# Another order within a step: local attention and FFN of a gated block on one core

## The chip, the cores and the metric

One core of a Trainium2 chip runs the whole program. The metric is device time in microseconds (us). The engines are TensorE (PE, with PEld for its weight loads), VectorE (DVE), ScalarE (ACT), GpSimd (POOL) and SyncE (SP, which issues DMAs here). Each engine works its own queue in order, and they meet at semaphores.

## The reference

The input x (2 batches of 2048 tokens, 256 wide) is normalised and goes through two branches; the result is `x + s * silu(ffn)`. The branch s is global attention of 16 heads. The change concerns the second branch, two layers of local attention and a gated feed-forward network:

```python
def _layer(x, wqkv, qs, ksc, wo, lg, lb, w1, b1, w2, b2):
    h = shift_token(x)                       # half of the features one token later
    q, k, v = jnp.split(h @ wqkv, 3, axis=-1)     # 8 heads of 64
    q = l2norm(q) * qs
    k = l2norm(k) * ksc
    q, k = rotary_xpos(q, k)
    o = local_attention(q, k, v)             # window of 128 and the one before it
    x = x + o @ wo
    h = shift_token(x)
    h = (h - mu) / jnp.sqrt(var + 1e-05) * lg + lb
    a, g = jnp.split(h @ w1 + b1, 2, axis=-1)     # 682 each
    h = a * jax.nn.gelu(g, approximate=False)
    return x + h @ w2 + b2
```

All data are float32.

## The kernel before

`norms` and `global_attention` run first; they are not changed. `ffn_branch` (lines 422 to 899) is the last stage.

**Tiling.** A *slot* is 512 tokens of one batch in one layer: 2 layers x 4 chunks x 2 batches = 16 slots, numbered s, with the two batches in turn. A slot has four *steps* i = 0 to 3, each for one tile of 128 tokens. x lies transposed in `xA` (features on partitions), with one column ahead of it for the token shift.

**Pieces.** The order of all engines' queues is the order in which the Python code emits, under `manual_schedule`; waits between engines follow from the tiles. A *piece* is one function call. `piece(f)` calls it, then counts down a list `later`: `soon(n, f)` puts f there, and it is emitted behind the n-th piece after the one that asked for it (n = 0: right behind that one). `gates` holds functions that are emitted once in a step, ahead of the first `a_weights`.

**Attention of one tile.** `a_project(s, i, n)` (544) multiplies by wqkv: n = 0 is q, 1 is k, 2 is v. For v, ACT copies the result out. For q and k, ACT squares it (`sqq`, 567), DVE makes three products from the same PSUM bank (`rot`, `swp`, 573 to 575), POOL adds them (576), and two pieces later `norm` emits DVE's sum of squares and maximum (580, 584), POOL's power -1/2 (585) and POOL's scaling of `rot` (586). In the next step `a_turn` (590) transposes rot on PE; ACT copies q out, DVE copies k. `a_scores(hb)` (612) makes the scores of four heads (hb 0 or 1) in two banks; DVE adds the mask and takes the maximum (636); `weights` on ACT is four exponentials (645); `normalize`, a piece later, is DVE's reciprocal (651) and two products on POOL (`sm`, 654). `a_weights(hb)` (659) transposes sm on PE into two banks (`pw`, r = 0 and 1), copied to `pT` by ACT for r = 0 and DVE for r = 1. `a_sums(hb)` (678) multiplies by v (`po`); at hb 1 ACT copies to `oT`. `a_out` (700, `px`) multiplies by wo and DVE adds it to xA (`residual`, 520).

**FFN of one slot.** `f_mean` (713, `pm`) gives the mean by a matmul, DVE subtracts it (`hc`), ACT squares it (725). `f_var` (727, `pv`) is the mean of the squares; its `scale` is ACT's square root (735), DVE's reciprocal of 128x512 (736) and DVE's scaling of hc (740, 741). `f_gate(m, n)` (747, `pg`): twelve pieces, Gelu on ACT for n = 1, product on DVE for n = 0. `f_out(k, part)` (771): in layer 1 two halves of a sum (`py`) and a residual on DVE, in layer 2 `pz`, an addition, Silu, and the product and sum with the other branch.

**PSUM.** `bank` (452) gives out eight banks in turn. A bank that comes round again is written only when all that read its last contents are done.

**The loop** (833 to 899). In step (s, i) `cur` is the tile that is projected and `pre` the one of the step before, for which all attention is done. FFN work comes from slots s-1 (`a_out`, `f_mean`, `f_var`), s-2 (gates) and s-3 (`f_out`), as `xs` and `gs`:

| step | xs | gates |
|---|---|---|
| 0 | f_out half 0, parts 0 and 1 | 4 |
| 1 | a_out 0 and 1 | 2 |
| 2 | f_out half 1, parts 0 and 1 | 2 |
| 3 | f_mean, f_var | 4 |

The order in a step is: turn 0, turn 1 of pre; q of cur; scores 0; k of cur; first xs; scores 1; second xs; v of cur; `gates`; weights 0; a gate; weights 1; a gate; sums 0; other gates; sums 1. `load_1` and `load_2` bring the FFN weights of layer 2 on SP's queue behind steps (9, 3) and (10, 2); `load_qkv` ahead of (8, 0).

Of the kernel before, what the change touches and what calls it, by code (L numbers as in the profile page):

```python
# [18 lines left out]
P = 128  # L19
# [402 lines left out]
def ffn_branch(tc, t, xA, s_out, ident, eps_t, mean_w, vecs, b2_row, x_ch, out_ch):  # L422
# [8 lines left out]
    with ExitStack() as ctx:  # L431
# [13 lines left out]
        )  # L445
        mhalf = cp.tile([P, H2], F32, name="mhalf")
        nc.gpsimd.memset(mhalf, -0.5)
        ctx.enter_context(tc.manual_schedule())

        turn = [0]  # L450

        def bank(name, shape=(P, CH)):
            turn[0] += 1
            return psr.tile(list(shape), F32, tag=f"f{turn[0] % 8}", name=name)
# [4 lines left out]
        def soon(n, f):  # L459
            later.append([n, f])  # L460

        def piece(f):
            f()
            for x in later:
                x[0] -= 1
            due = [x for x in later if x[0] < 0]
            later[:] = [x for x in later if x[0] >= 0]
            for _, g in due:
                g()


        W = {}
# [71 lines left out]
        def a_project(s, i, n):  # L544

            l, b, cc = slots[s]
            nm = f"{s}_{i}_{n}"
            ti = cc * TPC + i
            ps = bank(f"pp_{nm}")
            for k in range(2):  # L550
                at = ti * P + (1 if k == 0 else 0)
                nc.tensor.matmul(  # L552
                    ps, xA[b][:, k, at : at + P], W["qkv"][:, k, n * INNER : (n + 1) * INNER],
                    start=(k == 0), stop=(k == 1),
                )
            if n == 2:
                v = pool.tile([P, INNER], F32, tag=f"v{b}", name=f"v_{nm}", bufs=3)
                nc.scalar.copy(v, ps)
                kvs[l, b, ti, "v"] = v
                if i == 0:  # L560
                    soon(0, lambda: release("a", b))
                return
            if n == 0:
                st[s, i] = {"ss": pool.tile([P, 2, H2], F32, tag="ss", name=f"ss_{nm}"), "rot": []}
            S = st[s, i]
            sq = pool.tile([P, INNER], F32, tag="sqq", name=f"sqq_{nm}")
            nc.scalar.activation(sq, ps, AF.Square)  # L567
            rot = pool.tile([P, H2, HD2], F32, tag=f"rot{n}", name=f"rot_{nm}")
            swp = pool.tile([P, H2, HD2], F32, tag="swp", name=f"swp_{nm}")
            src = ps.rearrange("p (h d) -> p h d", d=HD2)  # L570
            hf = HD2 // 2
            tcs, tsn = (W["rt", x, cc][:, i, n, None, :] for x in range(2))
            nc.vector.tensor_mul(rot, src, tcs.to_broadcast([P, H2, HD2]))  # L573
            nc.vector.tensor_mul(swp[..., :hf], src[..., hf:], tsn[..., :hf].to_broadcast([P, H2, hf]))
            nc.vector.tensor_mul(swp[..., hf:], src[..., :hf], tsn[..., hf:].to_broadcast([P, H2, hf]))  # L575
            nc.gpsimd.tensor_add(rot, rot, swp)  # L576
            S["rot"].append(rot)

            def norm():
                nc.vector.tensor_reduce(  # L580
                    S["ss"][:, n, :], sq.rearrange("p (h d) -> p h d", d=HD2), AX.X, ALU.add
                )
                rn = pool.tile([P, H2], F32, tag="rn", name=f"rn_{nm}")
                nc.vector.tensor_scalar_max(rn, S["ss"][:, n, :], 1e-24)  # L584
                nc.gpsimd.tensor_tensor(rn, rn, mhalf, ALU.pow)  # L585
                nc.gpsimd.tensor_mul(rot, rot, rn[:, :, None].to_broadcast([P, H2, HD2]))

            soon(1, norm)
# [23 lines left out]
        def a_scores(s, i, hb):  # L612
# [25 lines left out]
                        mx[:, hb, r, x : x + 1],  # L638
                    )

            def weights():
                for r in range(2):
                    sm = S["sm"][hb, r]
                    for x in range(2):
                        nc.scalar.activation(  # L645
                            sm[:, x, lo:], sm[:, x, lo:], AF.Exp, scale=-1.0,
                            bias=mx[:, hb, r, x : x + 1], accum_out=ls[:, hb, r, x : x + 1],
                        )

            def normalize():  # L650
                nc.vector.reciprocal(ls[:, hb], ls[:, hb])  # L651
# [1 line left out]
                    sm = S["sm"][hb, r][:, :, lo:]  # L653
                    nc.gpsimd.tensor_mul(sm, sm, ls[:, hb, r, :, None].to_broadcast([P, 2, 2 * P - lo]))  # L654

            soon(0, weights)
            soon(1, normalize)

        def a_weights(s, i, hb):
# [4 lines left out]
            for r in range(2):  # L664
# [4 lines left out]
                            ps[:, x, pa, :], S["sm"][hb, r][:, x, pa * P : (pa + 1) * P], ident  # L669
                        )  # L670
                pT = pool.tile([P, 2, 2, P], F32, tag="pT", name=f"pT_{s}_{i}_{hb}_{r}", bufs=4)
                if r == 0:
                    nc.scalar.copy(pT[:, :, p0:, :], ps[:, :, p0:, :])
                else:
                    nc.vector.tensor_copy(pT[:, :, p0:, :], ps[:, :, p0:, :])  # L675
# [37 lines left out]
        def f_mean(s):  # L713
# [8 lines left out]
            release("f", b)  # L722
            sq = pool.tile([P, 2, CH], F32, tag="sq", name=f"sq_{s}", bufs=1)
            fs[s] = {"hc": hc, "sq": sq, "u": []}
            soon(0, lambda: nc.scalar.activation(sq, hc, AF.Square))

        def f_var(s):
            l, b, cc = slots[s]
# [2 lines left out]
            for k in range(2):  # L731
                nc.tensor.matmul(pw, mean_w, sq[:, k, :], start=(k == 0), stop=(k == 1))
            rs = pool.tile([P, CH], F32, tag="rs", name=f"rs_{s}", bufs=1)
            def scale():
                nc.scalar.activation(rs, pw, AF.Sqrt, bias=eps_t)
                nc.vector.reciprocal(rs, rs)
                V = vecs[:, l, :]
                for k in range(2):
                    c0 = 2 * NM + k
                    nc.vector.tensor_mul(hc[:, k, :], hc[:, k, :], rs)  # L740
                    nc.vector.tensor_scalar(
                        hc[:, k, :], hc[:, k, :], V[:, c0 : c0 + 1], V[:, c0 + 2 : c0 + 3], ALU.mult, ALU.add
                    )

            gates.append(scale)

        def f_gate(s, m, n):

# [3 lines left out]
            mw = min(P, HID - m * P)  # L752
            at = n * HID + m * P
            hc = fs[s]["hc"]
            ps = bank(f"pg_{nm}")
            for k in range(2):
                nc.tensor.matmul(  # L757
# [71 lines left out]
        load_2(0)  # L829
        n_slots = len(slots)  # L830
        per_layer = B * NCH
        last = None
        for s in range(n_slots + 3):
            a = s if s < n_slots else None

            fo, fg, fy = (x if 0 <= x < n_slots else None for x in (s - 1, s - 2, s - 3))
            for i in range(TPC):
                if i == 0 and s % B == 0 and B <= s <= per_layer:
                    if s == B:
                        load_scales(1)  # L840
                    load_tables(1, s // B - 1)
                if i == 0 and s == per_layer:
                    load_qkv(1)
                xs = []
                if i in (0, 2) and fy is not None:
                    xs = [(lambda p=p, k=i // 2: f_out(fy, k, p)) for p in range(2)]
                if i == 1 and fo is not None:
                    xs = [(lambda k=k: a_out(fo, k)) for k in range(2)]
                if i == 3 and fo is not None:
                    xs = [lambda: f_mean(fo), lambda: f_var(fo)]  # L850
                gs = []
                if fg is not None:
                    for m in ((0, 1), (2,), (3,), (4, 5))[i]:
                        gs += [(lambda m=m, n=n: f_gate(fg, m, n)) for n in (1, 0)]
                cur = (a, i) if a is not None else None
                pre = last
                last = cur

                def run(q, n=1):
                    for _ in range(n):  # L860
                        if q:
                            piece(q.pop(0))

                if pre:
                    piece(lambda: a_turn(*pre, 0))
                    piece(lambda: a_turn(*pre, 1))
                if cur:
                    piece(lambda: a_project(*cur, 0))
                if pre:
                    piece(lambda: a_scores(*pre, 0))  # L870
                if cur:
                    piece(lambda: a_project(*cur, 1))
                run(xs)
                if pre:
                    piece(lambda: a_scores(*pre, 1))
                run(xs)
                if cur:
                    piece(lambda: a_project(*cur, 2))
                for g in gates:
                    g()  # L880
                gates.clear()
                if pre:
                    piece(lambda: a_weights(*pre, 0))
                run(gs)
                if pre:
                    piece(lambda: a_weights(*pre, 1))
                run(gs)
                if pre:
                    piece(lambda: a_sums(*pre, 0))
                run(gs, 4)  # L890
                if pre:
                    piece(lambda: a_sums(*pre, 1))

                if s == per_layer and i == 1:
                    load_o(1)
                if s == per_layer + 1 and i == 3:
                    load_1(1)
                if s == per_layer + 2 and i == 2:
                    load_2(1)


# [87 lines left out]
```

## Time and profile before

| | us |
|---|---|
| median of 3 runs | 3884.55 (3881.63 to 3889.24) |
| the profiled execution's own time | 3884.26 |
| its span | 3882.5 |
| last stage: first matmul of the FFN branch to the end | 2092.34 to 3882.5 |

The page gives the busy time of each engine over the span. A window line gives, for a stretch of time, its length, busy time of PE, PEld, DVE, ACT and POOL with the instructions in brackets, the clock granted to PE (1.00 is full), the DMA share and GB/s. A wait line reads: engine and line that waited, what it waited for, us in total, times, longest. A timeline line reads: start, us, engine, line, operation, output <- input, shapes, how many in the group, and in square brackets the idle time ahead of it with what ended it. Matmul ends are modelled, so the time from the start of a group to the start of the next is the better measure of its length.

### The profile page before, as it was taken

The page shows a single profiled execution, that of the slowest core. Times are in us where ns is not written, and L with a number is a line of the kernel's source. Part 1 is how long each engine was busy: PE and PEld are TensorE (multiplying, and loading weights), DVE is VectorE, ACT ScalarE, POOL GpSimd, SP SyncE. Part 2 cuts the span into 40 slices and gives each one's busy share as a digit, 9 for nine tenths or more (in the row PEclk, how much of TensorE's full clock was granted, in tenths as well). Part 3 has the DMA queues.
Part 4 walks back from the last instruction along what each step waited for, and adds up shares of the span by engine and source line. Part 5 has one row for each costly group of instructions (what it writes and reads, how often), then busy time and mean ns, then how long its engine had stood idle before and what let it go on. Part 6 is the DMA issues. An engine that isn't in the chain of part 4 may idle for free.

```text
span 3882.5 us, 56277 instructions
## 1 busy us (share of the span) xinstructions
PE 3564.7 (92%) x21856; PEld 1688.3 (43%) x21856; DVE 2334.0 (60%) x4894; ACT 2063.8 (53%) x4170; POOL 1156.3 (30%) x978
## 2 busy tenths in 40 slices
PE   2999999999999999999996778888989999999998
PEld 1534334334343343434432444444444445555554
DVE  8767777777777777777751444545444444444442
ACT  1166666666666666666663344444444444444452
POOL 4011111111111111111113544445444435454441
PEclk9699999999999999999997899999999999999999
DMA  2000000000000000000002000000000000000001
GB/s 72 4 1 1 1 1 1 1 1 1 12 6 7 1 1 1 1 1 1 1 12 79 1 6 1 6 1 6 1 22 6 1 28 9 17 17 17 17 9 44
DMA packets 26172, 40.44 MB, mean 10 GB/s; under 512 B 3806, under 2 KB 19122, under 8 KB 25906
## 3 DMA queue, kind: packets, MB, share of 16 engines
q1 hardware_dynamic: 24466, 34.08, 2.6%
q8 instruction: 172, 2.82, 0.3%
q10 hardware_dynamic: 1440, 2.77, 0.2%
q14 instruction: 94, 0.77, 0.1%
HBM read 28.46 MB, written 8.39 MB: 9 GB/s over the span
## 4 chain that ended last, share of the span: by engine, by line
PE 76%; DVE 11%; ACT 5%; POOL 5%; issue 2%; DMA 1%; ACTq 0%; POOLq 0%; SPq 0%; DVEq 0%
PE pm L280 16%; PE po L335 12%; PE ps L316 11%; PE pg L757 7%; PE pp L552 6%; PE po L689 4%; DVE mx L283 3%; PE px L704 3%; PE pz L800 2%; POOL sm L654 2%; PE pw L668 2%; PE px L374 2%; PE pt L598 2%; ACT sm L645 2%; PE pp_wk L232 2%
## 5 line engine op out<-in xcount | busy, mean ns | idle before, releaser
L283 DVE TENSOR_REDUCE mx<-pm 128x1 f32<-128x512 f32 x2048 | 1285.6, 683 | 450.9 <-PE ps L316 429.9
L322 ACT ACTIVATE e<-ps 128x512 f32<-128x512 f32 x2048 | 1059.4, 607 | 466.2 <-PE ps L316 345.0
L280 PE MATMUL pm<-kT,qT 32*128 32x512 f32 x4096 | 1148.8, 639 | 0.8 <-DVE mx L283 0.8
L316 PE MATMUL ps<-qa,kT 32*128 32x512 f32 x4096 | 1116.5, 627 | 5.7 <-ACT e L322 4.8
L345 POOL TENSOR_TENSOR o<-o,part 128x512 f32<-128x512 f32 x224 | 283.5, 1266 | 1580.6 <-ACT part L344 1580.6
L280 PEld LDWEIGHTS pm<-kT,qT 32*128 32x128 f32 x4096 | 432.4, 188 | 435.4 <-DVE mx L283 338.5
L335 PE MATMUL po<-e,v 128*32 128x512 f32 x4096 | 492.5, 598 | 0.0
L316 PEld LDWEIGHTS ps<-qa,kT 32*128 32x128 f32 x4096 | 390.9, 183 | 154.6 <-ACT e L322 62.5
L576 POOL TENSOR_TENSOR rot<-rot,swp 128x512 f32<-128x512 f32 x128 | 162.4, 1269 | 797.5 <-DVE swp L575 757.7
L552 PE MATMUL pp<-wqkv,xA 128*128 128x512 f32 x768 | 379.9, 618 | 14.4 <-DMA wqkv<-in_wqkv_dram 14.4
L757 PE MATMUL pg<-hc,w 128*128 128x512 f32 (+1 forms) x768 | 379.8, 629 | 0.0
L645 ACT ACTIVATE sm<-sm,wmx 128x256 f32<-128x256 f32 (+1 forms) x512 | 250.4, 490 | 171.9 <-DVE wmx L636 171.2
L654 POOL TENSOR_TENSOR sm<-sm,wls 128x512 f32<-128x512 f32 (+1 forms) x256 | 254.2, 1014 | 26.6 <-DVE wls L651 23.7
L335 PEld LDWEIGHTS po<-e,v 128*32 128x32 f32 x4096 | 106.9, 109 | 348.1 <-DVE mx L283 187.4
L573 DVE TENSOR_TENSOR rot<-pp,rt 128x512 f32<-128x512 f32 x128 | 88.5, 691 | 248.7 <-ACT sqq L567 230.4
L585 POOL TENSOR_TENSOR rn<-rn,mhalf 128x8 f32<-128x8 f32 x128 | 210.8, 1647 | 55.4 <-DVE rn L584 55.4
L344 ACT COPY part<-po 128x512 f32<-128x512 f32 x224 | 131.0, 585 | 167.0 <-PE po L335 167.0
L689 PE MATMUL po<-pT,v 128*64 128x128 f32 x1984 | 159.3, 301 | 55.8 <-DVE pT L675 55.8
L552 PEld LDWEIGHTS pp<-wqkv,xA 128*128 128x128 f32 x768 | 138.7, 197 | 154.3 <-issue 141.2
L668 PE MATMUL pw<-ident,sm 128*128 128x128 f32 x992 | 150.0, 288 | 60.6 <-POOL sm L654 59.7
L675 DVE COPY pT<-pw 128x512 f32<-128x512 f32 (+1 forms) x128 | 84.8, 672 | 195.5 <-PE pw L668 195.4
L757 PEld LDWEIGHTS pg<-hc,w 128*128 128x128 f32 (+1 forms) x768 | 132.9, 187 | 142.0 <-issue 141.3
(136 smaller groups left out, 3795.8 us busy)
## 6 DMA issues: line engine op xcount, KB each, us to landing
xt<-in_x_dram SPq DMA_DIRECT2D x8, 512.0 KB, 3.7
s_out<-s_all SPq DMA_DIRECT2D x8, 512.0 KB, 2.6
rt<-in_rot_dram SPq DMA_DIRECT2D x16, 256.0 KB, 4.6
s<-s_out SPq DMA_DIRECT2D x16, 256.0 KB, 3.4
x<-in_x_dram SPq DMA_DIRECT2D x16, 256.0 KB, 3.5
out_dram<-y SPq DMA_DIRECT2D x16, 256.0 KB, 2.2
wqkv<-in_wqkv_dram SPq DMA_DIRECT2D x4, 768.0 KB, 8.3
w<-in_w_dram SPq DMA_DIRECT2D x4, 682.0 KB, 5.5
```

What stands on the lines that cost most here:

```text
L280: nc.tensor.matmul(ps, qT[rows, q0 : q0 + P], kT[rows, c * CH : (c + 1) * CH], start=True, stop=True)
L283: nc.vector.tensor_reduce(mxs[n][:, i * GH + j, c : c + 1], ps, AX.X, ALU.max)
L316: nc.tensor.matmul(ps, kT[rows, kt * P : (kt + 1) * P], qas[n][rows, :], start=True, stop=True)
L322: nc.scalar.activation(e, ps, AF.Exp)
L335: nc.tensor.matmul(pos[n][j * HP : (j + 1) * HP, :], v[:, kt, j * HP : (j + 1) * HP], es.pop((n, kt, j)), start=(kt % 2 == 0), stop=(kt % ...
L345: nc.gpsimd.tensor_add(os[n], os[n], part)
L552: nc.tensor.matmul(ps, xA[b][:, k, at : at + P], W["qkv"][:, k, n * INNER : (n + 1) * INNER], start=(k == 0), stop=(k == 1),)
L645: nc.scalar.activation(sm[:, x, lo:], sm[:, x, lo:], AF.Exp, scale=-1.0, bias=mx[:, hb, r, x : x + 1], accum_out=ls[:, hb, r, x : x + 1],)
L654: nc.gpsimd.tensor_mul(sm, sm, ls[:, hb, r, :, None].to_broadcast([P, 2, 2 * P - lo]))
L668: nc.tensor.transpose(ps[:, x, pa, :], S["sm"][hb, r][:, x, pa * P : (pa + 1) * P], ident)
L689: nc.tensor.matmul(S["po"][r * HD2 : (r + 1) * HD2, c, :], kvs[l, b, kt, "v"][:, h * HD2 : (h + 1) * HD2], S["pT", hb, r][:, x, pa, :], st ...
L757: nc.tensor.matmul(ps[:mw], W["1"][:, k, at : at + mw], hc[:, k, :], start=(k == 0), stop=(k == 1))
```

## The change

The diff does the following.

- A step has another order: sums 1 of the tile two steps back (`pre2`); v of cur; turn 0 and 1 of pre; the first of xs; scores 0 of pre; q of cur; scores 1; k of cur; the rest of xs; `gates`; weights 0; gates; weights 1; gates; sums 0; gates.
- FFN work is dealt out anew. xs is f_var(s-2) in step 0, two a_out(s-1) in step 1, f_out(s-3) half 0 in step 2, f_out half 1 and f_mean(s-1) in step 3. The gates of s-2 are queued from step 1 on, 2, 3, 2 and, in step 0 of the next slot, 5.
- `f_var`'s function becomes `root` (square root on ACT at once), `invert` (the reciprocal in four quarters, 1, 3, 5 and 7 pieces on) and `scale(k)` (10 and 11 pieces on). If hc isn't scaled at a gate, `all_due` emits all that is pending.
- The exponentials are emitted within `a_scores`, which is where `soon(0, ...)` had put them.
- The addition of the rotation (576) goes from POOL to DVE; the maximum with 1e-24 (584) is taken against a constant tile `tiny` instead of an immediate.
- `pT` is copied by DVE for hb 0 and by ACT for hb 1.
- The pending column of xA (`release("a")`) is written two pieces after k is projected. `load_1(1)` and `load_2(1)` move to behind (10, 0) and (10, 3).
- The steps behind the last tile have a plan of their own.

```diff
-            nc.gpsimd.tensor_add(rot, rot, swp)
+            nc.vector.tensor_add(rot, rot, swp)
...
-                nc.vector.tensor_scalar_max(rn, S["ss"][:, n, :], 1e-24)
+                nc.vector.tensor_max(rn, S["ss"][:, n, :], tiny)
...
-                if r == 0:
+                if hb == 1:
                     nc.scalar.copy(pT[:, :, p0:, :], ps[:, :, p0:, :])
...
-            soon(0, lambda: nc.scalar.activation(sq, hc, AF.Square))
+            soon(1, lambda: nc.scalar.activation(sq, hc, AF.Square))
...
-            def scale():
+            def root():
                 nc.scalar.activation(rs, pw, AF.Sqrt, bias=eps_t)
-                nc.vector.reciprocal(rs, rs)
+                for q in range(TPC):
+                    soon(2 * q + 1, lambda q=q: invert(q))
+                soon(2 * TPC + 2, lambda: scale(0))
+                soon(2 * TPC + 3, lambda: scale(1))
+
+            def invert(q):
+                nc.vector.reciprocal(rs[:, q * P : (q + 1) * P], rs[:, q * P : (q + 1) * P])
...
+            if not fs[s].get("ready"):
+                all_due()
...
+                if i == 0 and have(s - 2):
+                    xs = [lambda: f_var(s - 2)]
+                if i == 1 and have(s - 1):
+                    xs = [(lambda k=k: a_out(s - 1, k)) for k in range(2)]
+                if i == 1 and have(s - 2):
+                    gq += gate_pieces(s - 2)
+                if i >= 2 and have(s - 3):
+                    xs = out_pieces(s - 3, i - 2)
+                if i == 3 and have(s - 1):
+                    xs = xs + [lambda: f_mean(s - 1)]
+                ng = (5, 2, 3, 2)[i]
...
+            if pre2:
+                piece(lambda: a_sums(*pre2, 1))
+            if cur:
+                piece(lambda: a_project(*cur, 2))
+            if pre:
+                piece(lambda: a_turn(*pre, 0))
+                piece(lambda: a_turn(*pre, 1))
+            run(xs)
+            if pre:
+                piece(lambda: a_scores(*pre, 0))
+            if cur:
+                piece(lambda: a_project(*cur, 0))
+            if pre:
+                piece(lambda: a_scores(*pre, 1))
+            if cur:
+                piece(lambda: a_project(*cur, 1))
+                if i == 0:
+                    soon(2, lambda: release("a", slots[s][1]))
+            run(xs, 9)
+            for g in gates:
+                g()
+            gates.clear()
+            if pre:
+                piece(lambda: a_weights(*pre, 0))
+            run(gq, (ng + 1) // 3)
+            if pre:
+                piece(lambda: a_weights(*pre, 1))
+            run(gq, (ng + 1) // 3)
+            if pre:
+                piece(lambda: a_sums(*pre, 0))
+            run(gq, ng - 2 * ((ng + 1) // 3))
```

More of the change, by code (lines that the diff above doesn't have):

```diff
@@ L447, in ffn_branch @@
         nc.gpsimd.memset(mhalf, -0.5)
+        tiny = cp.tile([P, H2], F32, name="tiny")
+        nc.gpsimd.memset(tiny, 1e-24)
         ctx.enter_context(tc.manual_schedule())
@@ L469, in piece, with all_due @@
                 g()
+        def all_due():
+            while later:
+                later.pop(0)[1]()
         W = {}
@@ L559, in a_project @@
                 kvs[l, b, ti, "v"] = v
-                if i == 0:
-                    soon(0, lambda: release("a", b))
                 return
@@ L639, in a_scores @@
                     )
[L641 to L648, printed above, removed]
+            for r in range(2):
+                sm = S["sm"][hb, r]
+                for x in range(2):
+                    nc.scalar.activation(
+                        sm[:, x, lo:], sm[:, x, lo:], AF.Exp, scale=-1.0,
+                        bias=mx[:, hb, r, x : x + 1], accum_out=ls[:, hb, r, x : x + 1],
+                    )
             def normalize():
@@ L654, in normalize @@
                     nc.gpsimd.tensor_mul(sm, sm, ls[:, hb, r, :, None].to_broadcast([P, 2, 2 * P - lo]))
-            soon(0, weights)
             soon(1, normalize)
@@ L733, in f_var, with scale @@
             rs = pool.tile([P, CH], F32, tag="rs", name=f"rs_{s}", bufs=1)
-            def scale():
+            def root():
                 nc.scalar.activation(rs, pw, AF.Sqrt, bias=eps_t)
-                nc.vector.reciprocal(rs, rs)
-                V = vecs[:, l, :]
[L738 to L745, printed above, removed]
+                for q in range(TPC):
[4 more added lines that the diff above has]
+                nc.vector.reciprocal(rs[:, q * P : (q + 1) * P], rs[:, q * P : (q + 1) * P])
+            def scale(k):
+                c0 = 2 * NM + k
+                V = vecs[:, l, :]
+                nc.vector.tensor_mul(hc[:, k, :], hc[:, k, :], rs)
+                nc.vector.tensor_scalar(
+                    hc[:, k, :], hc[:, k, :], V[:, c0 : c0 + 1], V[:, c0 + 2 : c0 + 3], ALU.mult, ALU.add
+                )
+                fs[s]["ready"] = k == 1
+            gates.append(root)
         def f_gate(s, m, n):
@@ L831, in ffn_branch @@
         per_layer = B * NCH
[L832 to L899, printed above, removed]
@@ new lines, in out_pieces, with gate_pieces, have, run @@
+        def out_pieces(s, k):
+            return [(lambda p=p: f_out(s, k, p)) for p in range(2)]
+        def gate_pieces(s):
+            return [(lambda m=m, n=n: f_gate(s, m, n)) for m in range(NM) for n in (1, 0)]
+        gq = []
+        tiles = [(s, i) for s in range(n_slots) for i in range(TPC)]
+        for n in range(len(tiles) + 4):
+            s, i = divmod(n, TPC)
+            cur, pre, pre2 = (tiles[x] if 0 <= x < len(tiles) else None for x in (n, n - 1, n - 2))
+            def have(x):
+                return 0 <= x < n_slots
+            xs = []
+            if s == n_slots:
+                if i == 1:
+                    xs = [lambda: a_out(s - 1, 0), lambda: a_out(s - 1, 1)] + out_pieces(s - 3, 0)
+                    xs += [lambda: f_mean(s - 1)]
+                    gq += gate_pieces(s - 2)
+                elif i == 2:
+                    xs = out_pieces(s - 3, 1) + [lambda: f_var(s - 1)]
+                elif i == 3:
+                    xs = []
+                else:
+                    xs = [lambda: f_var(s - 2)]
+                ng = (5, 2, 5, 5)[i]
+            else:
+                if i == 0 and have(s - 2):
+                    xs = [lambda: f_var(s - 2)]
+                if i == 1 and have(s - 1):
+                    xs = [(lambda k=k: a_out(s - 1, k)) for k in range(2)]
+                if i == 1 and have(s - 2):
+                    gq += gate_pieces(s - 2)
+                if i >= 2 and have(s - 3):
[3 more added lines that the diff above has]
+                ng = (5, 2, 3, 2)[i]
+            if i == 0 and s % B == 0 and B <= s <= per_layer:
+                if s == B:
+                    load_scales(1)
+                load_tables(1, s // B - 1)
+            if i == 0 and s == per_layer:
+                load_qkv(1)
+            def run(q, n=1):
+                for _ in range(n):
+                    if q:
+                        piece(q.pop(0))
+            if pre2:
[29 more added lines that the diff above has]
+            run(gq, ng - 2 * ((ng + 1) // 3))
+            if s == per_layer and i == 1:
+                load_o(1)
+            if s == per_layer + 2 and i == 0:
+                load_1(1)
+            if s == per_layer + 2 and i == 3:
+                load_2(1)
@@ L903, in _padded_heads @@
+        s = n_slots + 1
+        run(gq, 99)
+        for k in range(2):
+            run(out_pieces(s - 3, k), 2)
+        gq += gate_pieces(s - 2)
+        run(gq, 3)
+        for g in gates:
+            g()
+        gates.clear()
+        run(gq, 99)
+        for k in range(2):
+            run(out_pieces(s - 2, k), 2)
+        all_due()
+        for g in gates:
+            g()
+        gates.clear()
 def _padded_heads(w):
```

## The prediction

> **What bounds the kernel now.** First the page's busy line and the windows over the span, to find the stage; then who TensorE waited for, from 2085 us on; then TensorE's timeline over one chunk; last the clock in the two stretches behind the long gaps.
>
> ```profile
> PE 3564.7 (92%) x21856; PEld 1688.3 (43%) x21856; DVE 2334.0 (60%) x4894; ACT 2063.8 (53%) x4170; POOL 1156.3 (30%) x978
> ```
>
> ```profile
> 2800.00:3000.00 200.00, 183.32 (x909) 95.26 (x908) 95.37 (x279) 91.33 (x211) 94.58 (x81) 0.95 0.04 14
> ```
>
> The change touches only the last stage (2092 to 3882 us). In it TensorE (PE) is busy 183 of 200 us, VectorE (DVE) 95, ScalarE (ACT) 91, GpSimd (POOL) 95: PE sets the pace, the others are half idle and matter only where PE waits for them.
>
> ```profile
> PE pv L732 <- ACT sq L725: 65.9, 16, 4.3
> PE pw L668 <- POOL sm L654: 59.7, 50, 4.2
> PE po L689 <- DVE pT L675: 55.8, 15, 5.5
> ```
>
> Three waits hold nearly all PE idle time: pv and po once a slot, pw mostly in the first slots, where no FFN work covers the softmax.
>
> ```profile
> 2770.29 1.09 PE L598 MATMUL pt<-ident,rot 128*128 128x128 f32 x8
> 2771.22 1.88 PE L552 MATMUL pp<-wqkv,xA 128*128 128x512 f32 x4
> 2773.03 1.16 PE L623 MATMUL ps<-xT,xT 64*128 64x128 f32 x16
> ...
> 2775.95 1.88 PE L718 MATMUL pm<-xA,mean_w 128*128 128x512 f32 x4
> 2777.76 1.16 PE L623 MATMUL ps<-xT,xT 64*128 64x128 f32 x16
> 2783.24 3.51 PE L732 MATMUL pv<-sq,mean_w 128*128 128x512 f32 x4 [4.32 <-ACT sq L725]
> ...
> 2797.59 1.76 PE L689 MATMUL po<-pT,v 128*64 128x128 f32 x13 [3.59 <-DVE pT L675]
> ```
>
> ```profile
> 2783.00:2786.60 3.60, 3.37 (x5) 1.53 (x6) 1.82 (x10) 2.26 (x9) 3.52 (x4) 0.54 0.00 0
> 2797.00:2806.00 9.00, 8.40 (x42) 4.12 (x43) 2.54 (x4) 1.00 (x2) 0.00 (x0) 0.64 0.01 2
> ```
>
> Both gaps lie in step 3, and behind each the granted clock is 0.54 and 0.64: pv takes 3.34 us to the next group where pm takes 1.81.
>
> A slot lasts 107.1 us (px at 2304.98 and, 13 slots on, 3697.40). Groups in the timeline, start to start at full clock: pp 1.82, ps 1.09, pw 0.88, half a po 0.95, pt 0.93, pg 1.8, px 3.6, py 2.66 and 2.97, pm and pv 1.8. Times the counts of a slot (12, 8, 8, 8, 4, 12, 2, 2 and 2, 1 and 1): 92.7 us. The other 14.4 are idle (8.3% of 107, 8.8 us) and slow clock.
>
> **What the Trainium skill says.** "SBUF — State Buffer", section on the two separate sides: VectorE with two SBUF inputs and GpSimd share a port pair under an exclusive lock; the loser blocks for the whole instruction. The trace agrees for the maximum on line 584: 0.17 us alone, but 0.90 here, until the first POOL product ends:
>
> ```profile
> 2144.68 2.05 POOL L654 TENSOR_TENSOR sm<-sm,wls 128x512 f32<-128x512 f32 x2
> 2144.86 0.90 DVE L584 TENSOR_SCALAR rn<-ss 128x8 f32<-128x8 f32 x1
> ```
>
> "PSUM — Partial Sum Buffer", its summary of rules: guard PSUM by bank, not by address. The trace agrees: with DVE free, the first mask starts at 3771.09, 0.14 us after the last ps of its pair of banks ended (3769.47 + 1.48).
>
> ```profile
> 3769.47 1.48 PE L623 MATMUL ps<-xT,xT 64*128 64x128 f32 x16 [0.24 <-ACT xT L601]
> ...
> 3771.09 0.42 DVE L636 CUSTOM_DVE_ANT_0 sm<-ps,mask 128x256 f32<-128x256 f32 x1 [1.13 <-PE ps L623]
> ```
>
> "TensorE: Matmul & The Clock Gate", on oscillation: PE idle beyond about 3.4 us brings back the half clock. The trace shows it behind 4.32 and 3.59; behind some gaps of 3.44 in the first slots pw x8 takes 2.11 instead of 1.04, behind others not.
>
> **The change, part by part.** Removed: pv's wait (f_var comes a step after f_mean), and po's wait (the 3.35 us reciprocal is cut in four quarters between pieces, the scaling put later). That is 4.3 + 3.6 us and, by the groups behind them, 1.6 + 2.6 of slow clock: 12.1 a slot. The 1.1 us pw waits of steps 0 and 2 would be next.
>
> Edits that cost nothing by themselves: POOL's addition (1.27 us, 128 times) leaves an engine half idle; DVE gains two additions a step, 0.69 each by the SBUF product on line 740, on 13 of 27 us, so DVE is no throughput bound. The maximum against `tiny` stays near 0.17 us plus the lock. Copies of pT change engine by half instead of by pair: same count. Weight loads for layer 2 move, but their last use moves with them and 15 us or more of pieces lie before the first use, against 5.5 to 8.3 us to land; next on SP's queue are the s and x loads of the output, two steps or more later. Table products on POOL stand at the same step start, before sm.
>
> What costs is the order. ACT's queue in a step is now exp0, square q, exp1, square k; DVE's is mask0, rotate q and add, reciprocal 0, mask1, rotate k and add, reciprocal 1, then the second FFN or px piece's residual. Each hands to the other, so it is one chain. From the end of scores 0 on PE (t = 0), with gaps from the timeline:
>
> - mask0 0.14; exp table at 0.65 (1.3); four exps 1.97: square q at 3.92.
> - rotation 0.60 later, 4.52 (the trace shows DVE waiting for the square every time); three products 1.27; addition 0.63: reciprocal 0 at 6.43.
> - POOL starts 0.32 after it: the first half of sm0 at 7.8, the second at 8.8.
> - mask1 6.5, exp1 0.46 later, four exps: square k 8.95; rotation 9.55; addition 10.82. POOL then ends its power (1.65) and starts the q product (1.04): the lock costs 0 or 1.05; neither end is excluded, I take 0.5. It ends 11.95.
> - reciprocal 1 11.95; POOL: sm1 halves 13.3 and 14.35. A residual (0.74) comes after it: 12.8.
>
> And eight PSUM banks go round in order of allocation. Counted off the new loop: py is followed by two score banks, q, two, k, and two pw banks; the second pw bank of hb 0 is py's own (in step 3, with pm between, the first). In step 0 it is pv's, which is free when ACT's Sqrt, now queued behind square k, ends: 9.5 + 1.3 (table) + 0.69 (line 735) = 11.5. So these transposes wait for the residual or the root, not only for sm. Before, py's bank came back at hb 1, long free.
>
> PE's cover from t = 0 and its waits, by step:
>
> - step 0: q 1.8, scores 1.1, k 1.8 = 4.7. sm0 at 7.85: 3.15. Then 8.3 to 11.5: 3.2.
> - step 1: with px 3.6, 8.3. sm0 is there (0.1). With pw and one gate 11.0; sm1 at 13.35 and 14.4: 2.9.
> - step 2: with py 2.95, 7.65, 0.2 for sm0; at 8.3 the bank, 12.8: 4.5.
> - step 3: with py and pm 9.45; bank 12.8: 3.35. The next half of po waits 0.6 for ACT's pT, behind Square (1.06) and Gelu.
>
> Sum 18.0; a slot is 92.7 + 18.0 = 110.7. Three gaps or pairs are near or over the 3.4 us behind which the clock fell; 1.6 us each (pv's loss), I take two: 3.2. Slot 113.9, 6.8 more than now; 13 slots: +88.
>
> Ends: in slots 0 to 2 the new chain lacks the exp table load (t = 13.1 for sm1) and a step comes to 22 us, as now (22.05, 22.9, 21.8); f_mean's and the reciprocal's waits of slots 1 and 2 go, five gates move out, step 1 of slot 1 loses its px cover: −5. The tail from the last tile on: five gates more (9), 5 us for the first softmax, less wait elsewhere: 126 against 114, +12. Sum +95 on the profiled execution's span of 3882.5 us (its own time 3884.26, 0.3 below the median): 3979; I say 3980.
>
> **Rivals.** *Cover as now, step 3 gains* (the faster case): if sm1 were ready 11 us after scores 0, as early as PE gets there, the 12.1 and some 1.5 of pw waits go: 13 × 13.6 − 7 = −170, 3715. For it: half of DVE and ACT is idle. Against: their order, above; it decides if the chain is 3.4 us shorter, which needs squares and rotations not to be waited for. *Chain without slow clock, DVE wins the lock*: slot 109.2, +34, 3918. For it: gaps are split by short groups. *Banks free early* (the count or the order of residuals misread): waits for sm alone, 13.2, slot 105.9: −9, 3875. Against: residuals stand behind both rotations in DVE's queue. *VectorE as bound*: excluded above.
>
> **How the numbers follow.** Forecast 0.52, its own range 3920 to 4040; no slow clock 0.20; banks free 0.13; step 3 gains in full or part (3700 to 3860) 0.15. A change of 0.2% (8 us) is about what can be told from none. Slower: 0.52 + 0.20 + 0.02 = 0.74; same 0.05; faster 0.21. The range 3850 to 4050 leaves out most of the faster case (0.13) and 0.07 above, where both lock and clock fall out badly.
>
> **What would show it.** Right: pv and po nearly gone from PE's waits; pw the largest by far, some 250 to 290 us, released in step 0 by the Sqrt or POOL, in steps 2 and 3 by the residual (lines of xA), in step 1 by POOL; PE's clock below 0.95; DVE additions of 0.69 with some near 1.7. Wrong: pw waits below 1 us in steady slots, or a slot below 107 us.

## The result and the profile after

The changed kernel takes 4032.93 us (median of 4 runs, 4029.47 to 4034.97), the kernel before 3885.88 beside it: ratio 1.0378, 95% interval 1.0361 to 1.0394. It is 147 us slower; 95 were forecast. The profiled execution's span is 4033.2 us, 150.7 more than before.

The page's line of busy times of the kernel after:

```profile
PE 3623.5 (90%) x21856; PEld 1721.1 (43%) x21856; DVE 2464.4 (61%) x5070; ACT 2053.4 (51%) x4166; POOL 1001.6 (25%) x851
```

TensorE executes the same 21856 matmuls and is busy 58.8 us longer. The last stage in one window line each, first the kernel before, then after:

```profile
2091.00:3883.00 1792.00, 1588.11 (x8096) 877.40 (x8096) 833.17 (x2292) 797.09 (x1765) 812.22 (x688) 0.94 0.04 14
```

```profile
2091.00:4033.00 1942.00, 1648.07 (x8096) 910.86 (x8096) 964.08 (x2468) 786.74 (x1761) 657.46 (x560) 0.90 0.04 13
```

The stage is 150 us longer: PE idle grew from 203.9 to 293.9 (+90), and its 8096 matmuls took 60 us longer at a mean clock of 0.90 instead of 0.94. Those two numbers are the whole loss. VectorE is 131 us longer busy and GpSimd 155 us less, but both stand idle for about half of the stage or more; they count only where TensorE waits for them.

Who PE waited for, in the kernel after, on the weights transpose:

```profile
PE pw L670 <- POOL sm L657: 126.5, 69, 4.5
PE pw L670 <- DVE xA L536: 65.0, 16, 4.6
PE pw L670 <- DVE y L822: 35.9, 10, 4.2
PE pw L670 <- ACT rs L737: 24.1, 8, 3.1
PE pw L670 <- POOL rot L590: 17.0, 6, 3.1
```

The waits of pv (65.9) and po (55.8) are gone. What is left in the steady slots is pw: 268.5 us over the stage, against 59.7 before. The names xA (layer 1's residual), y (layer 2's addition) and rs (the square root) are no inputs of a weights transpose. They are the last readers of the bank that it is about to write. "POOL rot" in step 0 is such a case with a wrong name: the product on POOL ended at 2861.71, but so, within 0.2 us, did the square root (2861.56), and it is the root that reads the bank.

```profile
2860.67 1.04 POOL L590 TENSOR_TENSOR rot<-rot,rn 128x512 f32<-128x512 f32 x1
...
2860.87 0.69 ACT L737 ACTIVATE rs<-pv,eps_t 128x512 f32<-128x512 f32 x1
```

PE's timeline of the kernel after, over steps 2, 3, 0 and 1 in turn:

```profile
2790.14 1.16 PE L627 MATMUL ps<-xT,xT 64*128 64x128 f32 x16
2791.24 1.98 PE L558 MATMUL pp<-wqkv,xA 128*128 128x512 f32 x4
2793.15 1.16 PE L627 MATMUL ps<-xT,xT 64*128 64x128 f32 x16
2794.24 1.99 PE L558 MATMUL pp<-wqkv,xA 128*128 128x512 f32 x4
2796.07 2.93 PE L793 MATMUL py<-u,w 128*128 128x512 f32 x6
2799.16 0.66 PE L670 MATMUL pw<-ident,sm 128*128 128x128 f32 x4 [0.16 <-POOL sm L657]
2804.38 1.09 PE L670 MATMUL pw<-ident,sm 128*128 128x128 f32 x4 [4.56 <-DVE xA L536]
2805.26 3.62 PE L769 MATMUL pg<-hc,w 128*128 128x512 f32 x4
...
2835.50 1.06 PE L670 MATMUL pw<-ident,sm 128*128 128x128 f32 x8 [3.60 <-DVE xA L536]
2836.40 3.14 PE L769 MATMUL pg<-hc,w 128*128 128x512 f32 x4
...
2857.91 1.12 PE L670 MATMUL pw<-ident,sm 128*128 128x128 f32 x4 [2.93 <-POOL sm L657]
2861.70 1.09 PE L670 MATMUL pw<-ident,sm 128*128 128x128 f32 x4 [2.67 <-POOL rot L590]
2862.58 6.09 PE L769 MATMUL pg<-hc,w 128*128 128x512 f32 x8
...
2897.44 0.65 PE L670 MATMUL pw<-ident,sm 128*128 128x128 f32 x4 [2.32 <-POOL sm L657]
2898.44 1.12 PE L670 MATMUL pw<-ident,sm 128*128 128x128 f32 x4 [0.34 <-POOL sm L657]
2899.35 3.07 PE L769 MATMUL pg<-hc,w 128*128 128x512 f32 x4
```

Every step now ends its projections with a gap ahead of pw: together 16.6 us in the slot shown (16.2 on average over twelve). Behind each, four pg that take 1.8 us at full clock take 2.9 to 3.4, and eight, 3.4 at full clock, take 5.9. A slot (pm to pm, from 2471.80 to 3893.43 over twelve) is 118.5 us; before it was 107.0. Twelve slots give 137 of the 150.7 us, the ends 13.

The chain behind the 4.56 us gap of step 2, from the timeline of the kernel after, all engines:

```profile
2791.34 0.42 DVE L640 CUSTOM_DVE_ANT_0 sm<-ps,mask 128x256 f32<-128x256 f32 x1 [2.97 <-PE ps L627]
...
2795.12 0.57 ACT L571 ACTIVATE sqq<-pp 128x512 f32<-128x512 f32 x1
...
2797.73 0.17 DVE L654 RECIPROCAL wls<-wls 128x4 f32<-128x4 f32 x1
...
2800.23 0.57 ACT L571 ACTIVATE sqq<-pp 128x512 f32<-128x512 f32 x1
...
2801.92 1.04 POOL L590 TENSOR_TENSOR rot<-rot,rn 128x512 f32<-128x512 f32 x1
2802.22 1.28 DVE L580 TENSOR_TENSOR rot<-rot,swp 128x512 f32<-128x512 f32 x1
...
2803.52 0.72 DVE L536 SCALAR_TENSOR_TENSOR xA<-py,vecs,xA 128x512 f32<-128x512 f32 x1
```

py itself ended near 2799. Its residual started at 2803.52, because on DVE it stands behind both rotations, and these wait for squares that stand behind exponentials on ACT. The second addition takes 1.28 us, the first 0.69: the second runs beside POOL's product, which ends at 2802.96.

### The profile page after: what moved, and what is told of

The parts are those of the page before. It is cut to its first block, busy times and chain, and to the rows that moved or that the text cites. A ratio compares the mean times of both kernels' runs of the same rounds, so it can differ in the third digit from the quotient of the medians.

```text
span 4033.2 us, 56293 instructions
## 1 busy us (share of the span) xinstructions
PE 3623.5 (90%) x21856; PEld 1721.1 (43%) x21856; DVE 2464.4 (61%) x5070; ACT 2053.4 (51%) x4166; POOL 1001.6 (25%) x851
## 5 line engine op out<-in xcount | busy, mean ns | idle before, releaser
L769 PE MATMUL pg<-hc,w 128*128 128x512 f32 (+1 forms) x768 | 438.4, 710 | 4.3 <-DVE hc L750 3.7
L670 PE MATMUL pw<-ident,sm 128*128 128x128 f32 x992 | 186.4, 332 | 270.1 <-POOL sm L657 126.5
L558 PE MATMUL pp<-wqkv,xA 128*128 128x512 f32 x768 | 385.5, 625 | 14.3 <-DMA wqkv<-in_wqkv_dram 14.3
L670 PEld LDWEIGHTS pw<-ident,sm 128*128 128x128 f32 x992 | 138.7, 170 | 380.7 <-issue 186.6
L640 DVE CUSTOM_DVE_ANT_0 sm<-ps,mask 128x256 f32<-128x256 f32 (+1 forms) x512 | 180.3, 408 | 128.2 <-PE ps L627 128.2
L335 PEld LDWEIGHTS po<-e,v 128*32 128x32 f32 x4096 | 107.0, 109 | 348.1 <-DVE mx L283 187.4
L577 DVE TENSOR_TENSOR rot<-pp,rt 128x512 f32<-128x512 f32 x128 | 88.5, 691 | 241.8 <-ACT sqq L571 221.6
L769 PEld LDWEIGHTS pg<-hc,w 128*128 128x128 f32 (+1 forms) x768 | 156.7, 222 | 171.9 <-issue 165.6
L608 DVE COPY xT<-pt 128x512 f32<-128x512 f32 x64 | 44.3, 691 | 293.7 <-PE pt L602 293.7
L778 DVE SCALAR_TENSOR_TENSOR u<-pg,vecs,gl 128x512 f32<-128x512 f32 x96 | 72.0, 749 | 229.9 <-PE pg L769 219.9
```

The source lines that it names most:

```text
L335: nc.tensor.matmul(pos[n][j * HP : (j + 1) * HP, :], v[:, kt, j * HP : (j + 1) * HP], es.pop((n, kt, j)), start=(kt % 2 == 0), stop=(kt % ...
L558: nc.tensor.matmul(ps, xA[b][:, k, at : at + P], W["qkv"][:, k, n * INNER : (n + 1) * INNER], start=(k == 0), stop=(k == 1),)
L670: nc.tensor.transpose(ps[:, x, pa, :], S["sm"][hb, r][:, x, pa * P : (pa + 1) * P], ident)
L769: nc.tensor.matmul(ps[:mw], W["1"][:, k, at : at + mw], hc[:, k, :], start=(k == 0), stop=(k == 1))
```

## Experiments

Times are medians of 4 runs; the kernel before was 3883 to 3888 beside each. Slot lengths are pm to pm over the steady slots, as above.

**E1: pass over the FFN piece's bank.** `bank` keeps a list and skips the bank of py, pz or pv until weights 1 are emitted.

```diff
...
+            n = next(x for x in ring if x not in held_banks)
+            ring.remove(n)
+            ring.append(n)
+            if hold:
+                held_banks.append(n)
...
-                    F["py"] = bank(f"py_{s}_{k}")
+                    F["py"] = bank(f"py_{s}_{k}", hold=True)
...
                 piece(lambda: a_weights(*pre, 1))
+            held_banks.clear()
```

> The changed kernel, but a bank taken by the step's FFN piece (py, pz or pv) is passed over in the round until weights 1 are emitted, so that no weights transpose (pw) needs the residual, the output's addition or the Sqrt. Chain and banks (my account): the waits of pw on those three (125 us together) go, waits on sm take part of their place (some 13 us a slot are left of 16.6), time falls by 40 to 75 us, to about 3975. Rival 'the bank is only the last name' (sm1 comes as late anyway): pw waits as long as before, now on sm: within 10 us of 4033.

Measured: 3915.48, 117 us less; ratio to the kernel before 1.0079 (1.0064 to 1.0094). A slot is 109.4 us. The timeline of E1 over steps 0 and 2:

```profile
2819.56 0.65 PE L674 MATMUL pw<-ident,sm 128*128 128x128 f32 x4 [2.94 <-POOL sm L661]
2820.56 1.11 PE L674 MATMUL pw<-ident,sm 128*128 128x128 f32 x4 [0.34 <-POOL sm L661]
2821.47 4.66 PE L773 MATMUL pg<-hc,w 128*128 128x512 f32 x8
...
2874.49 0.65 PE L674 MATMUL pw<-ident,sm 128*128 128x128 f32 x4 [0.17 <-POOL sm L661]
2875.48 0.66 PE L674 MATMUL pw<-ident,sm 128*128 128x128 f32 x4 [0.34 <-POOL sm L661]
...
2880.18 0.66 PE L674 MATMUL pw<-ident,sm 128*128 128x128 f32 x4 [2.33 <-POOL sm L661]
```

The banks were a cause, not a name for something that came late anyway: the first pw of step 2 now waits 0.5 us in all. What is left is sm alone, 10.8 us a slot instead of 16.6. The gain is larger than expected because the time lost to the slow clock falls with the gaps: what lies above the prediction's 92.7 us of matmuls and the waits is 5.9 us a slot here, 9.2 in the changed kernel, and the mean clock over twelve slots is 0.96 instead of 0.91.

**E2: reciprocal and POOL's products right behind the exponentials.**

```diff
-            soon(1, normalize)
+            normalize()
```

> The changed kernel, but the reciprocal and the two POOL products of a half stand right behind its exponentials, ahead of the rotation that follows. Chain and banks: sm0 is ready some 2 us and sm1 some 3 us earlier; step 1 (2.7 us of wait and 1.7 of slow clock) and the first slots gain, steps 0, 2, 3 stay bound by the banks: 60 to 110 us less, about 3945. Rival 'sm alone sets it': 3 us in every step, 190 us less, about 3845. Rival 'the DVE addition and the port lock cost the time': no gain.

Measured: 3999.43, 34 us less, below all that was expected of a gain. sm waits fell from 126.5 to 43.0 us, as meant, but those for the banks rose from 142.0 to 196.5. **E7** below is the same edit in the other order, where it made things worse, and shows why.

**E3: the addition back on GpSimd**, that line alone.

```diff
-            nc.vector.tensor_add(rot, rot, swp)
+            nc.gpsimd.tensor_add(rot, rot, swp)
```

> The changed kernel with the rotation's addition back on GpSimd, that edit alone undone. Chain and banks: DVE's part is 1.9 us shorter, so the residual frees the bank earlier, but POOL's additions put sm1 about 0.9 us later, and it binds instead: between -25 and +15 us. Rival 'the addition and the lock cost the time': at least 60 us less.

Measured: 3968.77, 64 us less: the rival's number. The second pw of step 2 starts 11.0 us after scores 0 instead of 13.1, near the expected 1.9 earlier. sm1 is later, as expected: POOL starts its product 13.11 us after scores 0, 12.46 in the changed kernel. But it doesn't bind in place of the bank. In steps 2 and 3 a gate stands ahead of weights 1 and covers it: weights 1 wait for nothing in step 2 and 0.27 + 0.34 us in step 3. So most of the gain stays, and some of the slow clock goes with it. E3's timeline, steps 2 and 3:

```profile
2786.61 1.09 PE L670 MATMUL pw<-ident,sm 128*128 128x128 f32 x4 [2.13 <-DVE xA L536]
...
2814.72 1.06 PE L670 MATMUL pw<-ident,sm 128*128 128x128 f32 x8 [1.55 <-DVE xA L536]
```

4.56 became 2.13 and 3.60 became 1.55. Whether the addition costs by itself or through the bank is what E6 asks.

**E6: E1 and E3 together.**

> E1 (banks passed over) and E3 (addition on GpSimd) together. If the addition on VectorE costs only by way of the bank that waits for the residual behind it, it is worth nothing once the bank is not waited for: 3905 to 3930, as E1. If it has a price of its own (VectorE's time, the port lock), E3's 64 us come on top: about 3850.

Measured: 3963.42. With the banks passed over the addition on GpSimd is not worth 64 us but costs 48 (3963.42 against E1's 3915.48); VectorE's addition has no price of its own that shows. It lengthens the chain to the residual and shortens POOL's queue ahead of sm; which of the two counts depends on what PE waits for. Here PE waits for sm alone, 225.8 us against 189.9 in E1. Neither of the two expected values came.

**E4: the old order, with everything else of the change kept** (f_var a step later, quartered reciprocal, gates 2, 3, 2, 5, addition on VectorE).

```diff
             if pre2:
                 piece(lambda: a_sums(*pre2, 1))
-            if cur:
-                piece(lambda: a_project(*cur, 2))
             if pre:
                 piece(lambda: a_turn(*pre, 0))
                 piece(lambda: a_turn(*pre, 1))
-            run(xs)
+            if cur:
+                piece(lambda: a_project(*cur, 0))
             if pre:
                 piece(lambda: a_scores(*pre, 0))
             if cur:
-                piece(lambda: a_project(*cur, 0))
+                piece(lambda: a_project(*cur, 1))
+            run(xs)
             if pre:
                 piece(lambda: a_scores(*pre, 1))
+            run(xs, 9)
             if cur:
-                piece(lambda: a_project(*cur, 1))
+                piece(lambda: a_project(*cur, 2))
                 if i == 0:
-                    soon(2, lambda: release("a", slots[s][1]))
-            run(xs, 9)
+                    soon(0, lambda: release("a", slots[s][1]))
```

> The new FFN plan (f_var a step after f_mean, quartered reciprocal, 2, 3, 2, 5 gates, addition on DVE) with the order of before within a step (turns, q, scores 0, k, first xs, scores 1, other xs, v). Order as the cause: step 3's waits are gone and pw waits 2 to 4 us a slot, mostly in step 0: slot 95 to 97 us, total 3740 to 3800, below both kernels. Rival 'the new FFN plan or the addition costs the time': 3900 or more.

Measured: 3799.95, 86 us below the kernel before (ratio 0.9781, 0.9767 to 0.9796) and 233 below the changed one. The total is at the upper edge of what was expected, and a slot, 100.8 us, is above the expected 95 to 97. This parts the change in two: everything in it but the order, the new FFN plan above all, gains 2.2%; the order on top of it loses 6%. PE's largest wait in E4, where no wait for a bank is left:

```profile
PE pw L670 <- POOL sm L657: 125.9, 93, 4.5
```

The largest one in a steady slot is 2.79 us in step 0, where f_var is the only FFN piece ahead of the weights.

**E5: more work for TensorE.** Transposes of the identity into the bank that pw writes next, in two of the gaps of the changed kernel.

```diff
                 ps = bank(f"pw_{s}_{i}_{hb}_{r}", (P, 2, 2, P))
+                if r == 0 and s > 0 and (i, hb) in ((3, 0), (0, 1)):
+                    for _ in range(24 if hb == 0 else 18):
+                        nc.tensor.transpose(ps[:, 0, 1, :], ident, ident)
```

> The changed kernel with work added on TensorE and nothing else: ahead of the first weights transpose, 24 transposes of the identity into its own bank in step 0 (hb 0, gap 2.93 us) and 18 in step 1 (hb 1, gap 2.32 us), 2.6 and 2.0 us by the 0.11 us of one; the output is the same. If the groups behind a gap are long because TensorE stood idle (slow clock, my account), step 1 loses its 1.7 us and step 0 some 1 to 2 of its 3.2: 2.5 to 4 us a slot, 35 to 60 us less, about 3985, with the waits themselves filled and not shortened. If they are long for another reason, the time stays within 10 us of 4033 or grows.

Measured: 3999.41, 34 us less with some 69 us more of matmuls (15 slots of 4.6). A slot is 116.1 us, 2.4 less. The waits of PE in E5:

```profile
PE pw L673 <- DVE xA L536: 65.1, 16, 4.6
PE pw L673 <- POOL sm L657: 64.1, 71, 4.1
```

The residual's waits, which weren't filled, are as they were to 0.1 us, so the chain on the other engines gained nothing; what changed is the clock behind the filled gaps. In step 1 of E5, behind 18 transposes:

```profile
2881.75 0.66 PE L673 MATMUL pw<-ident,sm 128*128 128x128 f32 x4 [0.36 <-POOL sm L657]
...
2883.24 1.88 PE L772 MATMUL pg<-hc,w 128*128 128x512 f32 x4
```

In step 1 the four pg take 1.8 us in all twelve steady slots; unfilled they took 2.7 to 3.0 in ten of the twelve. There, idle time is what made the group behind it slow. Step 0 is less clear: of its gap a wait of 3.13 us for the bank remains, and the eight pg fall to 3.4 us in three of the twelve slots and stay above 5 in nine. In the last three of the twelve a slot takes some 119.5 us with and without the filling.

**E7: E4 with E2's edit.**

> E4 (old order, new FFN plan) with the reciprocal and POOL's products right behind the exponentials. Here sm alone is waited for, so it should gain where the same edit gained little in the new order: step 0's 3.1 us and its slow clock, the 1.4 us of steps 1 and 2, and 2 to 3 us in each of the first nine steps: 60 to 100 us less, 3700 to 3740. If the waits were for something else than sm, no gain beyond 15 us.

Measured: 3841.67, 42 us more than E4. The timeline of E7 and who the rotation waited for in E4 and in E7:

```profile
2738.65 0.57 ACT L571 ACTIVATE sqq<-pp 128x512 f32<-128x512 f32 x1
...
2738.78 0.18 DVE L654 RECIPROCAL wls<-wls 128x4 f32<-128x4 f32 x1 [2.45 <-ACT sm L648]
2738.88 0.66 DVE L584 TENSOR_REDUCE ss<-sqq 128x8 f32<-128x512 f32 x1
```

```profile
  ACT sqq L571: 212.1, 126
```

```profile
  ACT sqq L571: 93.4, 63
```

In E4 nearly every rotation (126 of 128) found DVE idle and waited for its square. In E7 half of them don't. The reciprocal now holds DVE's queue for 2.45 us. The sum of squares and the maximum, which had been done while DVE waited for the next square (`norm` is emitted one piece after its projection), come after the reciprocal and push the rotation, the mask and the Sqrt that follow: waits for the Sqrt's bank, none in E4, are 48.2 us. The wait was for sm, but a wait moved forward in a queue in order takes along what is queued behind it. E2's small gain has the same cause: waits of the rotation for its square fall from 221.6 us (125 times) in the changed kernel to 23.0 (63).

**E8: E4 with the addition on GpSimd.**

> E4 with the rotation's addition on GpSimd, as it was. Chain: DVE's part gets 0.6 to 1.9 us shorter, POOL has 1.27 us more ahead of sm, as before the change: pw waits about the same, within 25 us of E4, 3775 to 3825. Rival 'the addition costs 64 us in any order': 3736.

Measured: 3796.79, the same as E4 (3799.95) within the runs. Taking the addition back to GpSimd gains 64 us, loses 48 or does nothing, by its surroundings.

**E9 and E10: gates ahead of the first weights transpose**, in E1 and in E4.

```diff
...
+                plan = ((2, 1, 2), (1, 1, 0), (1, 1, 1), (1, 1, 0))[i]
...
+            run(gq, plan[0])
             if pre:
                 piece(lambda: a_weights(*pre, 0))
...
```

> E1 (new order, banks passed over) with gates moved ahead of the first weights transpose: two in step 0, one in each other step, taken from those behind it. If the new order loses because too little TensorE work lies between the scores and the weights, 1.8 us of cover a gate takes the waits of 2.3 us in steps 1 and 2 to about 0.5 and those of 2.9 and 1.4 in steps 0 and 3 to nothing, with most of the slow clock: 9 to 12 us a slot, 110 to 145 us less than 3915, about 3790. If the chain moves with the cover (banks or pT copies wait instead), less than 40 us.

Measured: 3916.02, no gain over E1. PE's idle time did fall, from 10.3 to 8.6 us a slot on average: the waits for sm went from 189.9 to 127.2 us, and po took 35.3 for pT copies on DVE. But the matmuls of a slot took 1.9 us longer. Step 3 shows it:

```profile
2804.13 0.43 PE L695 MATMUL po<-pT,v 128*64 128x128 f32 x2 [2.01 <-DVE pT L681]
2804.73 3.94 PE L695 MATMUL po<-pT,v 128*64 128x128 f32 x30 [0.17 <-DVE pT L681]
```

In E1 all 32 matmuls of a po take 1.9 us; here thirty take 3.9 behind the new wait. And step 0's wait moved from the first pw (2.94) to the second (2.33). In E1 PE reached that second one 14.3 us after scores 0, when sm1 is ready anyway. Cover ahead of a wait gains nothing where the wait moves on to the next group and takes the slow clock along.

> E4 (old order, new FFN plan) with the same gates moved ahead. Step 0's wait of 3.1 us and the 1.5 us of slow clock behind it go, and most of the 1.4 us in steps 1 and 2: 5 to 7 us a slot, 60 to 90 us less than 3800, about 3725. If po now waits for the copies of pT instead (sums 0 follow weights 1 directly in steps 1 and 3), less than 30 us.

Measured: 3775.69, 24 us less than E4. The waits of E10:

```profile
PE pw L670 <- POOL sm L657: 54.6, 30, 4.0
PE pg L769 <- ACT rs L737: 43.4, 13, 3.3
```

sm's wait in the steady slots is gone (0.5 us over twelve), and a gate in step 0 runs into the bank that the Sqrt reads. So the gain was small for another reason than the one expected: po waits only 9.0 us for pT.

**E11: E10 with E1's banks.**

> E10 (old order, new FFN plan, gates ahead) with the banks passed over as in E1. E10's largest wait in the steady slots is a gate that waits for the Sqrt that reads its bank (43 us, 3.3 a slot, and slow clock behind it). If the bank is the reason, that wait and some 1.7 us of slow clock a slot go: 40 to 65 us less than 3776, about 3720. If the Sqrt is late for what comes next anyway, less than 15 us.

Measured: 3753.27, 22 us less than E10: between the two expectations. The Sqrt's wait is gone, but 1.7 us of sm stand behind it in step 0. Its ratio to the kernel before is 0.9664 (0.9648 to 0.9681), the fastest of all: 131 us below before, 280 below the changed kernel. E9 and E11 differ in the order alone, with the banks passed over and the gates ahead in both: the order is worth 163 us there.

## Why the prediction was right, and where its size was off

- *Waits of step 3 removed, 12.1 us a slot.* Right: pv and po are gone from PE's waits, and E4, with that plan and the old order, is 86 us faster than before. A slot of E4 is 6.2 us shorter and not 12.1, since waits for sm, 5.4 us, take part of the place.
- *The chain ACT and DVE.* Right to some tenths: from the end of scores 0 (2791.3), square q was put at 3.92 and came at 3.8, reciprocal 0 at 6.43 and 6.43, square k at 8.95 and 8.9, the end of the residual at 12.8 and 12.9. The second addition was 0.6 us longer beside POOL's product, where 0.5 was taken between 0 and 1.05.
- *The banks.* Right: 4.5, 3.35 and 3.2 were worked out for steps 2, 3 and 0, and 4.56, 3.60 and 2.67 came. E1 shows them to be worth 117 us.
- *Waits in sum.* 18.0 us a slot predicted, 16.6 measured (the 0.6 of po in step 3 didn't come); pw 250 to 290 us, measured 268.5.
- *The slow clock* is the term that was mis-sized: "1.6 us each (pv's loss), I take two: 3.2". Measured: 118.5 - 92.7 - 16.6 = 9.2 us a slot, an average. By the same sum it is some 10 in a full slot with py and some 8 in one with pz, which takes about 2.8 us more than py. (The listed groups add to 92.6, which changes nothing.) All four gaps were followed by slow groups, the 2.3 us one of step 1 too, and behind step 0's pair the loss was near 3 us. A slot grew by 11.5 us where 6.8 were forecast: 6.0 more of slow clock, 1.4 less of waits. The step that was too mild is the rule that only gaps near or over 3.4 us cost clock: two were counted where four had to be. The result, 4033, lies 7 us inside the upper end of the stated 3920 to 4040.
- *The ends.* -5 at the start and +12 from the last tile on were predicted, and both came. The second px of slot 1 starts at 2299.69 instead of 2304.91 (5.2 us earlier), and from the last tile's turn to the end it takes 126.0 us instead of 114.4. But the sum has a hole: thirteen slots from 2304.98 end at 3697.40, and the 71 us from there to the last tile's turn (3768.14) are in no term. The thirteen slots grew by 139.2 us, that stretch by 5.0.
- *VectorE's addition at no cost of its own.* Right by E6 and E8; but as a part of the chain to the bank undone alone it gives back 64 of the 147 us, which the prediction's sum contains and doesn't name as such. The expectation for E3 had a gap of its own: sm1 came 0.65 us later (0.9 expected), but with a gate ahead of weights 1 that doesn't bind in steps 2 and 3.
- *Rivals.* Banks free early is excluded by the xA, y and rs waits. E1 makes that case by force, and its price of 3875 lacked the slow clock too: E1 waits 10.8 us a slot for sm (13.2 in the rival) and takes 3915. Cover as now is what E4 has and the new order lacks.

Left open: why the same gap of 2.33 us in step 1 of E1 is followed by slow groups in one slot (four pg 2.44 us) and not in the next (1.81), as it alternates over four slots. It wasn't followed further. Nor was the order taken apart: what v ahead of the turns and what the first FFN piece ahead of scores 0 cost by themselves, no run shows.

## What to carry to other kernels

Where an in-order pipeline loops through several engines, count the work that lies on the bounding engine between a chain's head and its tail, step by step; an order that starts the chain later with the same tail loses cover. Count the round of banks as well: a buffer's last reader may stand far back in another engine's queue, and the wait then bears a name that has no part in the data. And price a gap on TensorE at more than its length: here 90 us more idle brought 60 us more of slow matmuls, and E9, with less idle in more places, gained nothing.

## What the runs showed of the hardware

- Gaps shorter than the 3.4 us of the prediction's rule can bring the slow clock; the measurement decides. It isn't a matter of one gap's length alone: 2.32 with 0.34 us was followed by it here, a gap of 2.33 in E1 only in some slots. The clock of the changed kernel in four stretches behind gaps of 4.56, 3.60, 2.93 with 2.67, and 2.32 with 0.34:

```profile
2804.30:2809.90 5.60, 5.52 (x16) 3.38 (x17) 2.62 (x4) 0.78 (x2) 4.18 (x4) 0.53 0.00 0
2835.40:2840.70 5.30, 5.20 (x21) 3.33 (x22) 4.61 (x8) 1.27 (x2) 4.07 (x4) 0.68 0.00 0
2857.80:2868.50 10.70, 7.91 (x16) 3.98 (x17) 8.08 (x17) 5.01 (x10) 8.45 (x8) 0.54 0.00 1
2897.40:2902.30 4.90, 4.52 (x12) 2.34 (x12) 2.15 (x3) 1.17 (x2) 3.66 (x3) 0.65 0.00 0
```

- Matmuls of no use in such gaps made the kernel 34 us faster (E5).
- VectorE's sum of two SBUF tiles took 0.69 us at the least; in the changed kernel the median of its 128 times is 0.98 and the longest 1.60, and the one shown above beside GpSimd's product took 1.28. The maximum that the prediction shows has only one SBUF input; against `tiny` it has two, and beside POOL's product sm it takes 0.90 us as well, 0.17 alone:

```profile
2804.93 0.90 DVE L588 TENSOR_TENSOR rn<-ss,tiny 128x8 f32<-128x8 f32 x1
```

"SBUF — State Buffer", section on the two separate sides, states the exclusive lock for two SBUF inputs; these numbers agree.
